# A two-layer decoder on one core: the last routing's softmax, counts and ranks placed behind the slot products, three row normalisations given to GpSimd, and two pieces per head in the last four heads

## The chip, the cores and the metric

The kernel runs on one core of a Trainium2 chip. The metric is device time in microseconds: the median of three runs. One execution was also taken by the hardware profiler, and its page and trace are what this document reads. PE is TensorE's matmul, PEld its weight load, DVE is VectorE, ACT is ScalarE, POOL is GpSimd and SP is SyncE, which issues most of the DMAs.

## The reference, cut to what matters

The program is a decoder of two layers over 16 batches of 112 tokens with 256 features, with a context of 375 rows per batch. Each layer is self attention, cross attention and a mixture of experts. The change lies at the end of layer 1's cross attention and the start of its experts:

```python
# layer 1, experts: E = 8 experts, top 2, capacity 33 slots per batch and expert
logits = einsum('btc,ce->bte', x, router_w) + router_b
top_k_logits, expert_indices = top_k(logits, 2)
expert_probs = softmax(top_k_logits)
one_hot = one_hot(expert_indices, first choices before second choices)
pos = cumsum(one_hot, axis=0) * one_hot - 1          # place of a token in its expert's queue
expert_inputs = zeros((E, 33, C)).at[expert, pos].add(x)
h = expert_inputs @ w_c_fc + b_c_fc ;  g = expert_inputs @ w_gate + b_gate
o = silu(h * g) @ w_c_proj + b_c_proj
x = x + sum_k expert_probs[k] * o[expert_k, pos_k]
```

In the actual reference, x at this place is the layer's residual, and a place beyond the capacity is dropped on the way in and clamped to the last slot on the way out.

## The kernel before, in words

The residual `x` stays in SBUF as 112 partitions (tokens) by 16 batches by 256. The stages run one after the other, and all of them are built from matmuls with f32 operands whose results go through eight PSUM banks, handed out in turn by `bank()`. A bank that has not been emptied by DVE or ACT holds the next matmul that wants it.

**Cross attention of layer 1.** A loop of 32 units goes over 16 batches and two halves of the heads (`n`, `b`, `u`; a unit is called a head below). In each unit, PE turns the softmax of this unit (`turned`, L1493), computes the scores of the next unit (`scores`, L1461), then does pieces of other work, and last the values of this unit (`values`, L1509). DVE takes the row maxima (L1472) and reciprocals of the sums (L1482), ACT takes the exponentials (L1473), and POOL scales the four rows of probabilities (L1484), two after each reciprocal. The other pieces are: context normalisation and K, V and Q of the next batch (no K and V in heads before batches 4, 8 and 12, for which they were made earlier), the output product of the batch before (`project`, which adds into `x` at L1315 and takes statistics at L234 and L235; POOL makes the inverse deviation with L242 and L243, and DVE normalises at L238), its transposes into `xnT` (L267, L269), and one entry of the list `after`.

**The list `after`.** It holds functions, and each head pops one. `routed(b)` computes the router's logits of a batch (`logits1`, L1219). With every fourth batch it also runs `route1`, which takes the two largest logits of four batches (`top_two`, L297 to L305), the softmax of the two (L1227 to L1231), and returns `places`. `places` multiplies the one-hots by a triangular matrix on PE and then works on DVE: the position (L1250), the expert (L1252), whether it fits (`ok`, L1253), the clamped position `kept` (L1255), the slot number `place` (L1257 to L1259), and how many tokens lie beyond the first 12 slots (`more`, L1261, added to `need` at L1264). `dispatch1(b)` makes a 112x264 row of slots (`slot_rows`, L1285 and L1286), normalises the rows of the batch (L238), multiplies them on PE (L1275) and copies the result into `first_in` (first 12 slots of each expert) and `more_in` (the rest), once by DVE and once by ACT (L1278, L1279). What is still in the list behind the last head is done there, and the last routing, of batches 12 to 15, at the start of the expert stage.

**Experts.** The expert stage works by units of eight slots (`hidden(n, j)`): four matmuls (L120), one ACT step (L1766), one DVE product (L1767) and, for every second slot, a Silu. Units `(0, e)` take the first 12 slots of an expert, units `(1, r)` the remaining 21 of the expert of rank `r`. `ranks()` sorts the experts by `need`; its result is first used by the weight load and the biases of unit 2. A list `jobs` holds DVE work that fits beside the matmuls: biases by rank (`bias_of`), and the share matrices of the output (`share_jobs`). One job is popped per slot.

**What sets the order.** In the cross attention, only PE keeps the order in which the code issues (`manual_schedule` with PE alone); DVE's, ACT's and POOL's orders are set by a scheduler from its own estimate when the program is built. In the expert stage, PE and DVE keep the order of the code. Each engine then takes its queue strictly in order, whatever waits at its head.

Of the kernel before, what the change touches and what calls it, by code (L numbers as in the profile page):

```python
# [9 lines left out]
F32 = mybir.dt.float32  # L10
U32 = mybir.dt.uint32
AF = mybir.ActivationFunctionType
ALU = mybir.AluOpType
# [16 lines left out]
P0 = 12  # L30
# [8 lines left out]
def _constants():  # L39
# [28 lines left out]
        "rev16": rows(E0 - np.arange(E0)),  # L68
        "rev8": rows(E1 - np.arange(E1)),
        "io8": rows(np.arange(E1)),  # L70
        "slots": rows(np.arange(E1 * CAP)),

        "later": np.concatenate(
            [
# [24 lines left out]
def tile_decoder(ctx: ExitStack, tc: tile.TileContext, t: dict, out: bass.AP):  # L99
# [1121 lines left out]
    def route1(lp, q):  # L1221

        bs = slice(4 * q, 4 * q + 4)
        (oh0, v0), (oh1, v1) = top_two(lp, lg1[:, bs, :], E1, const("rev8", L))

        p0, ex = prob[0][:, bs], prob[1][:, bs]
        nc.vector.tensor_sub(ex, v1, v0)  # L1227
        nc.scalar.activation(ex, ex, AF.Exp)
        nc.vector.tensor_scalar(p0, ex, 1.0, None, ALU.add)
        nc.vector.reciprocal(p0, p0)  # L1230
        nc.vector.tensor_mul(ex, ex, p0)  # L1231

        oh = [o.rearrange("p b n -> p (b n)") for o in (oh0, oh1)]

        def places():
            pc = bank()
            before = const("before", L)
            mm_sum(pc[:L, : 4 * E1], [(before, oh[0])])
            mm_sum(pc[:L, 4 * E1 : 8 * E1], [(before, oh[1]), (ones[:L, :L], oh[0])])
            b1 = lambda name: lp.tile([L, 4], F32, tag=f"rt_{name}", name=name, bufs=1)  # L1240
            tmp = lp.tile([L, 4, E1], F32, tag="rt_tmp", name="tmp", bufs=1)
            sums = lp.tile([L, E1], F32, tag="rt_sums", name="sums", bufs=1)
            for k in range(2):
                pos, ok, more = b1(f"pos{k}"), b1(f"ok{k}"), b1(f"more{k}")
                o3 = (oh0, oh1)[k]
                kept, ei = pos1[k][:, bs], exp1[k][:, bs]
                nc.vector.tensor_tensor(
                    tmp, o3, pc[:L, 4 * k * E1 : 4 * (k + 1) * E1].rearrange("p (b n) -> p b n", n=E1), ALU.mult
                )
                nc.vector.tensor_reduce(pos, tmp, AX.X, ALU.add)  # L1250
                nc.vector.tensor_tensor(tmp, o3, over(const("io8", L), 4), ALU.mult)
                nc.vector.tensor_reduce(ei, tmp, AX.X, ALU.add)  # L1252
                nc.vector.tensor_scalar(ok, pos, CAP - 0.5, None, ALU.is_lt)  # L1253

                nc.vector.tensor_scalar(kept, pos, float(CAP - 1), None, ALU.min)  # L1255

                nc.vector.scalar_tensor_tensor(pos, ei, float(CAP), kept, ALU.mult, ALU.add)  # L1257
                nc.vector.scalar_tensor_tensor(pos, pos, 1.0, ok, ALU.add, ALU.mult)
                nc.vector.tensor_scalar(place[k][:, bs], pos, -1.0, None, ALU.add)  # L1259

                nc.vector.tensor_scalar(more, kept, P0 - 0.5, None, ALU.is_gt)  # L1261
                nc.vector.tensor_tensor(tmp, o3, bcast(more, E1), ALU.mult)
                nc.vector.tensor_reduce(sums, tmp.rearrange("p b n -> p n b"), AX.X, ALU.add)
                nc.vector.tensor_add(need, need, sums)  # L1264

        return places

    def dispatch1(lp, b, made=None):

# [8 lines left out]
            copy(first_in[:, c, :, :, b], src[:, :, :P0])  # L1278
            copy(more_at[:, c, :, :, b], src[:, :, P0:])  # L1279

    def slot_rows(lp, b):
        slots = const("slots", L)
        dm = lp.tile([L, E1 * CAP], F32, tag="dm", name="dm", bufs=2)
        d1 = lp.tile([L, E1 * CAP], F32, tag="d1", name="d1", bufs=1)
        nc.vector.tensor_scalar(d1, slots, place[0][:, b : b + 1], None, ALU.is_equal)  # L1285
        nc.vector.scalar_tensor_tensor(dm, slots, place[1][:, b : b + 1], d1, ALU.is_equal, ALU.add)  # L1286
        xn = lp.tile([L, D], F32, tag="xn", name="xn", bufs=2)
        normed(xn, x[:, b, :], mv1[:, b, 0:1], r1[:, b : b + 1])
        return dm, xn


# [5 lines left out]
    with ExitStack() as ph:  # L1297
# [243 lines left out]
        with tc.manual_schedule(engines={mybir.EngineType.PE}):  # L1541
# [48 lines left out]
            def routed(b):  # L1590
                logits1(b)
                if b % 4 == 3:
                    q = b // 4
                    places = route1(rp, q)
                    after.append(places)
                    if q < B // 4 - 1:
                        after.extend(lambda b=b: dispatch1(lp, b) for b in range(4 * q, 4 * q + 4))

            units = [(b, u) for b in range(B) for u in range(2)]
            for n, (b, u) in enumerate(units):  # L1600
# [8 lines left out]
                if b + 1 in AHEAD and u == 0:  # L1609
                    k_load(b + 1)  # L1610
                    v_load(b + 1)
                if after:
                    after.pop(0)()
                if late and n:
                    flush(0)
                    if b:
# [29 lines left out]
    with ExitStack() as ph:  # L1646
# [261 lines left out]
```

## Time and profile before

| quantity | value |
|---|---|
| time, median of 3 runs | 1604.29 us (1603.69 to 1607.48) |
| the profiled execution's own time | 1611.35 us |
| span in the profile | 1609.6 us, mean granted clock 0.973 |
| PE, DVE, ACT, POOL busy | 1501.8, 964.1, 577.9, 483.1 us |
| last scores of the cross attention (L1461) | 1298.65 us from the span's start |
| last logits (L1219) | 1325.21 us |
| first slot row of the last routing (L1285) | 1333.43 us |
| first expert matmul | 1342.73 us |

The span is what the trace covers; the profiled execution took 1.75 us more than its span and about 7 us more than the median of the runs. A row of the timeline gives the start in us, the duration, the engine, the line of the kernel, the operation and, in brackets, how long the engine had been idle and what ended that. Durations of several instructions merged in a row are from the first start to the last end.

### The profile page before, as it was taken

How to read it: one execution, taken by the hardware profiler on the slowest of the kernel's cores; microseconds unless marked ns; L12 is line 12 of the kernel's file. 1: busy time of each engine (PE TensorE's matmuls, PEld its weight loads, DVE VectorE, ACT ScalarE, POOL GpSimd, SP SyncE). 2: the span in 40 equal slices, each digit the busy share in tenths (PEclk: the TensorE clock that was granted, in tenths of full speed). 3: DMA queues.
4: the chain of work that ended last, by engine and by line, in shares of the span. 5: the costliest groups of instructions: out<-in, count | busy, mean ns of one | idle time of the engine just before them, and what ended most of it. 6: DMA issues, size and time to landing. Idle time of an engine off the chain costs nothing.

```text
span 1609.6 us, 30346 instructions
## 1 busy us (share of the span) xinstructions
PE 1501.8 (93%) x11438; PEld 1127.5 (70%) x11438; DVE 964.1 (60%) x2649; ACT 577.9 (36%) x1437; POOL 483.1 (30%) x647
## 2 busy tenths in 40 slices
PE   7898999999988896899999989999999978999998
PEld 5776777777754585778888756666666657788786
DVE  6986777777762353976677655566575566342124
ACT  3441444444442252223333233343434323333332
POOL 5642122222115352323333344544445420000000
PEclk9999999999999897999999999999999988999999
DMA  6500322222224476200000010101010012344421
GB/s 170 143 10 21 94 67 65 67 65 65 64 76 158 130 231 214 54 24 1 1 1 2 20 56 10 49 20 48 19 30 30 1 53 79 137 178 157 147 89 48
DMA packets 84929, 116.52 MB, mean 72 GB/s; under 512 B 13433, under 2 KB 70946, under 8 KB 84778
## 3 DMA queue, kind: packets, MB, share of 16 engines
q1 hardware_dynamic: 78690, 98.25, 20.1%
q0 software_dynamic: 3312, 8.54, 1.6%
q10 hardware_dynamic: 2776, 7.72, 1.4%
q8 instruction: 95, 1.56, 0.4%
q14 instruction: 56, 0.46, 0.1%
HBM read 84.41 MB, written 22.08 MB: 66 GB/s over the span
## 4 chain that ended last, share of the span: by engine, by line
PE 76%; DVE 13%; POOL 4%; DMA 3%; issue 2%; another core or an unknown queue 1%; ACT 1%; SPq 0%; POOLq 0%; DVEq 0%; ACTq 0%
PE pT L120 49%; PE pT L785 3%; PE pT L1461 3%; PE pT L1493 2%; POOL pr L1484 2%; DVE mx L769 2%; PE pT L1509 2%; PE pT L803 2%; PE pT L767 2%; PE pT L1358 2%; PE pT L1393 2%; PE pT L1379 2%; PE pT L620 1%; DVE st L234 1%
## 5 line engine op out<-in xcount | busy, mean ns | idle before, releaser
L1484 POOL TENSOR_SCALAR pr<-pr,den 112x375 f32<-112x375 f32 x128 | 157.0, 1244 | 176.9 <-DVE den L1482 157.7
L120 PE MATMUL pT<-xnT,w_all 128*128 128x224 f32 (+2 forms) x800 | 165.3, 358 | 0.6 <-DVE xnT L269 0.5
L120 PEld LDWEIGHTS pT<-xnT,w_all 128*128 128x128 f32 x800 | 145.9, 197 | 10.2 <-issue 5.7
L794 ACT ACTIVATE pr<-pT 125x336 f32<-125x336 f32 x256 | 94.6, 456 | 126.3 <-PE pT L785 126.3
L769 DVE TENSOR_REDUCE mx<-pT 112x1 f32<-112x375 f32 x256 | 122.2, 539 | 11.3 <-PE pT L767 9.9
L1371 POOL TENSOR_TENSOR pr<-pr,den 112x448 f32<-112x448 f32 x64 | 59.9, 956 | 198.8 <-DVE den L1369 147.9
L120 PE MATMUL pT<-w_all 128*128 (+3 forms) x376 | 113.1, 453 | 1.7 <-ACT w_all L392 0.8
L120 PE MATMUL pT<-w_all,cT 128*125 128x256 f32 (+1 forms) x336 | 111.4, 475 | 0.0
L120 PE MATMUL pT<-cT,w_all 128*128 128x375 f32 x320 | 110.2, 486 | 0.0
L120 PE MATMUL pT<-w_all,xnT 128*112 128x256 f32 (+1 forms) x320 | 105.7, 477 | 1.9 <-ACT xnT L566 0.9
L120 PE MATMUL pT<-w_all,oT 128*112 128x256 f32 x448 | 106.4, 383 | 0.6 <-DVE oT L1400 0.6
L242 POOL TENSOR_SCALAR nr<-nmv 112x1 f32<-112x1 f32 x96 | 22.3, 232 | 273.7 <-DVE nmv L235 273.1
L1308 ACT COPY pT<-pT 112x448 f32<-112x448 f32 (+1 forms) x64 | 34.0, 532 | 170.9 <-PE pT L1493 88.3
L120 PEld LDWEIGHTS pT<-w_all 128*128 128x128 f32 (+2 forms) x376 | 70.2, 190 | 33.8 <-issue 4.6
L1473 ACT ACTIVATE pr<-pT,top 112x375 f32<-112x375 f32 x128 | 72.4, 572 | 56.8 <-DVE top L1472 54.4
L120 PEld LDWEIGHTS pT<-cT,w_all 128*128 128x128 f32 x320 | 59.3, 190 | 41.1 <-issue 5.8
L120 PEld LDWEIGHTS pT<-w_all,oT 128*112 128x112 f32 x448 | 75.7, 177 | 16.3 <-DVE oT L1400 1.0
L120 PE MATMUL pT<-first_in,w_all 128*128 128x192 f32 x512 | 86.6, 329 | 0.0
L120 PEld LDWEIGHTS pT<-first_in,w_all 128*128 128x128 f32 x512 | 84.4, 192 | 1.5 <-issue 0.3
L120 PEld LDWEIGHTS pT<-w_all,cT 128*125 128x125 f32 x336 | 61.1, 187 | 33.3 <-issue 22.7
L120 PEld LDWEIGHTS pT<-w_all,xnT 128*112 128x112 f32 x320 | 57.1, 183 | 35.8 <-issue 22.4
L1767 DVE SCALAR_TENSOR_TENSOR hT<-pT,vT,gt 128x192 f32<-128x192 f32 x64 | 26.7, 417 | 90.5 <-ACT gt L1766 90.4
(306 smaller groups left out, 3019.2 us busy)
## 6 DMA issues: line engine op xcount, KB each, us to landing
w_all<-in_L_ffn_w_c_fc_dram SPq DMA_DIRECT2D x12, 1024.0 KB
w_all<-in_L_ffn_w_gate_dram SPq DMA_DIRECT2D x12, 1024.0 KB
w_all<-in_L_ffn_w_c_proj_dram SPq DMA_DIRECT2D x12, 1024.0 KB
cx<-in_ctx_dram SPq DMA_DIRECT2D x32, 375.0 KB
kz<-kn SPq DMA_DIRECT2D x128, 46.9 KB
xg<-w_all SPq DMA_DIRECT2D x1, 5547.0 KB
xb<-xg SPq DMA_DIRECT2D x36, 129.0 KB
yb<-yo SPq DMA_DIRECT2D x16, 224.0 KB
```

The lines of the kernel that those rows point to most:

```text
L120: mm(o, l, r, start=(i == 0), stop=(i == len(terms) - 1))
L767: mm(ps[i][:L, :S], qz[b % 2][r, g, :], kz[b % 2][r, g, :], start=True, stop=True)
L769: nc.vector.tensor_reduce(mx[b % 2][:, g, i, 16:17], ps[i][:L, :S], AX.X, ALU.max, negate=True)
L785: mm(pw[i][:KC, j * L : (j + 1) * L], kz[b % 2][r, g, j * KC : (j + 1) * KC], qm[r, :], start=True, stop=True,)
L794: nc.scalar.activation(pr[:, i, :], pw[i][:KC, : NKC * L], AF.Exp)
L803: mm(po[32 * i : 32 * i + 32, :L], va[b % 2][:, j, 4 * g + i, :], pr[:, i, j * L : (j + 1) * L], start=(j == 0), stop=(j == NKC - 1),)
L1308: nc.scalar.copy(dst, src)
L1358: mm(ps[k][:L, s * L : (s + 1) * L], q, kk, start=True, stop=True)
L1371: nc.gpsimd.tensor_tensor(pr[:, k], pr[:, k], bcast(den[:, k, :], L), ALU.mult)
L1461: mm(ps[2 * s + k][:L, :S], qTs[b // 2][rows(k), m, (b % 2) * L : (b % 2 + 1) * L], kTs[b][rows(k), m, :], start=True, stop=True,)
L1473: nc.scalar.activation(pr[:, i, :], ps[i][:L, :S], AF.Exp, bias=top[:, i : i + 1], scale=1.0, accum_out=den[:, i : i + 1],)
L1484: nc.gpsimd.tensor_scalar(pr[:, n, :], pr[:, n, :], den[:, n : n + 1], None, ALU.mult)
```

## The change

- The slot constant gets one more entry, and slot numbers count from 1, so that a token that doesn't fit has number 0 and no subtraction of 1 is needed. `place` is made from the unclamped position and `ok`.
- `kept`, the clamped position, is computed by POOL.
- `route1` returns two functions. `places` keeps what the slot rows need. `counts` has the softmax, `more`, and the sums into `need`. For the first three routings, `counts` is an entry of `after` of its own, behind the four dispatches. For the last one it is the first entry of `jobs`, in the first slot of the first expert unit.
- From head 28 on, two entries of `after` are popped per head.
- At the start of the expert stage, POOL normalises the rows of batches 12, 13 and 14 (into three buffers); for batch 15, the copy that its transposes read is used.
- `ranks()` moves from in front of the last dispatches into the jobs, as the fifth, followed by the biases of rank 0.

```diff
-        "slots": rows(np.arange(E1 * CAP)),
+        "slots": rows(np.arange(E1 * CAP + 1)),
...
-        p0, ex = prob[0][:, bs], prob[1][:, bs]
-        nc.vector.tensor_sub(ex, v1, v0)
-        nc.scalar.activation(ex, ex, AF.Exp)
-        nc.vector.tensor_scalar(p0, ex, 1.0, None, ALU.add)
-        nc.vector.reciprocal(p0, p0)
-        nc.vector.tensor_mul(ex, ex, p0)
...
-                nc.vector.tensor_scalar(kept, pos, float(CAP - 1), None, ALU.min)
-
-                nc.vector.scalar_tensor_tensor(pos, ei, float(CAP), kept, ALU.mult, ALU.add)
-                nc.vector.scalar_tensor_tensor(pos, pos, 1.0, ok, ALU.add, ALU.mult)
-                nc.vector.tensor_scalar(place[k][:, bs], pos, -1.0, None, ALU.add)
-
-                nc.vector.tensor_scalar(more, kept, P0 - 0.5, None, ALU.is_gt)
-                nc.vector.tensor_tensor(tmp, o3, bcast(more, E1), ALU.mult)
+                to = place[k][:, bs]
+                nc.vector.scalar_tensor_tensor(to, ei, float(CAP), pos, ALU.mult, ALU.add)
+                nc.vector.scalar_tensor_tensor(to, to, 1.0, ok, ALU.add, ALU.mult)
+
+                nc.gpsimd.tensor_scalar(kept, pos, float(CAP - 1), None, ALU.min)
+
+        def counts():
+
+            p0, ex = prob[0][:, bs], prob[1][:, bs]
+            nc.vector.tensor_sub(ex, v1, v0)
+            nc.scalar.activation(ex, ex, AF.Exp)
+            nc.vector.tensor_scalar(p0, ex, 1.0, None, ALU.add)
+            nc.vector.reciprocal(p0, p0)
+            nc.vector.tensor_mul(ex, ex, p0)
...
+            for k in range(2):
+                more = b1(f"more{k}")
+                nc.vector.tensor_scalar(more, pos1[k][:, bs], P0 - 0.5, None, ALU.is_gt)
+                nc.vector.tensor_tensor(tmp, (oh0, oh1)[k], bcast(more, E1), ALU.mult)
                 nc.vector.tensor_reduce(sums, tmp.rearrange("p b n -> p n b"), AX.X, ALU.add)
                 nc.vector.tensor_add(need, need, sums)
 
-        return places
+        return places, counts
...
-    def slot_rows(lp, b):
-        slots = const("slots", L)
+    def slot_rows(lp, b, xn=None):
+        slots = const("slots", L)[:, 1:]
...
-        xn = lp.tile([L, D], F32, tag="xn", name="xn", bufs=2)
-        normed(xn, x[:, b, :], mv1[:, b, 0:1], r1[:, b : b + 1])
+        if xn is None:
+            xn = lp.tile([L, D], F32, tag="xn", name="xn", bufs=2)
+            normed(xn, x[:, b, :], mv1[:, b, 0:1], r1[:, b : b + 1])
...
-                    places = route1(rp, q)
+                    places, counts = route1(rp, q)
                     after.append(places)
                     if q < B // 4 - 1:
                         after.extend(lambda b=b: dispatch1(lp, b) for b in range(4 * q, 4 * q + 4))
+                    after.append(counts)
...
-                if after:
-                    after.pop(0)()
+                for _ in range(2 if n > 27 else 1):
+                    if after:
+                        after.pop(0)()
...
             late.pop(0)()
-            while after:
+            xns = {}
+            for b in range(B - 4, B - 1):
+                xns[b] = lp.tile([L, D], F32, tag="xn", name="xn", bufs=3)
+                nc.gpsimd.tensor_scalar(
+                    xns[b], x[:, b, :], mv1[:, b, 0:1], r1[:, b : b + 1], ALU.subtract, ALU.mult
+                )
+            xns[B - 1] = xn15
+            after.pop(0)()
+            while len(after) > 1:
                 after.pop(0)()
-            made = {b: slot_rows(lp, b) for b in (B - 4, B - 3)}
-            ranked = ranks()
+            made = {b: slot_rows(lp, b, xns[b]) for b in (B - 4, B - 3)}
             for b in range(B - 4, B):
                 dispatch1(lp, b, made.pop(b))
                 if b + 2 < B:
-                    made[b + 2] = slot_rows(lp, b + 2)
-            jobs = bias_of(0)
-            jobs += share_jobs(share_first, KA, first_idx)
+                    made[b + 2] = slot_rows(lp, b + 2, xns[b + 2])
+            ranked = []
+            jobs = [after.pop(0)] + share_jobs(share_first, KA, first_idx)
+            jobs.insert(4, lambda: ranked.extend(ranks()))
+            jobs[5:5] = bias_of(0)
```

More of the change, by code (lines that the diff above doesn't have):

```diff
@@ L1241, in places @@
             tmp = lp.tile([L, 4, E1], F32, tag="rt_tmp", name="tmp", bufs=1)
-            sums = lp.tile([L, E1], F32, tag="rt_sums", name="sums", bufs=1)
             for k in range(2):
-                pos, ok, more = b1(f"pos{k}"), b1(f"ok{k}"), b1(f"more{k}")
+                pos, ok = b1(f"pos{k}"), b1(f"ok{k}")
                 o3 = (oh0, oh1)[k]
@@ L1253, in places @@
                 nc.vector.tensor_scalar(ok, pos, CAP - 0.5, None, ALU.is_lt)
-                nc.vector.tensor_scalar(kept, pos, float(CAP - 1), None, ALU.min)
-                nc.vector.scalar_tensor_tensor(pos, ei, float(CAP), kept, ALU.mult, ALU.add)
-                nc.vector.scalar_tensor_tensor(pos, pos, 1.0, ok, ALU.add, ALU.mult)
-                nc.vector.tensor_scalar(place[k][:, bs], pos, -1.0, None, ALU.add)
-                nc.vector.tensor_scalar(more, kept, P0 - 0.5, None, ALU.is_gt)
-                nc.vector.tensor_tensor(tmp, o3, bcast(more, E1), ALU.mult)
+                to = place[k][:, bs]
[9 more added lines that the diff above has]
+            nc.vector.tensor_mul(ex, ex, p0)
+            b1 = lambda name: lp.tile([L, 4], F32, tag=f"rt_{name}", name=name, bufs=1)
+            tmp = lp.tile([L, 4, E1], F32, tag="rt_tmp", name="tmp", bufs=1)
+            sums = lp.tile([L, E1], F32, tag="rt_sums", name="sums", bufs=1)
+            for k in range(2):
+                more = b1(f"more{k}")
+                nc.vector.tensor_scalar(more, pos1[k][:, bs], P0 - 0.5, None, ALU.is_gt)
+                nc.vector.tensor_tensor(tmp, (oh0, oh1)[k], bcast(more, E1), ALU.mult)
                 nc.vector.tensor_reduce(sums, tmp.rearrange("p b n -> p n b"), AX.X, ALU.add)
                 nc.vector.tensor_add(need, need, sums)
-        return places
+        return places, counts
     def dispatch1(lp, b, made=None):
```

## The prediction

> **What bounds the kernel now.** I read the page first (busy rows, slices), then busy time by stretch, then the timeline of the stretches that the edit touches, and last the changed program's order of instructions on each engine with what each waits for.
>
> The page says that TensorE sets the pace nearly everywhere:
>
> ```profile
> span 1609.6 us, 30346 instructions
> PE 1501.8 (93%) x11438; PEld 1127.5 (70%) x11438; DVE 964.1 (60%) x2649; ACT 577.9 (36%) x1437; POOL 483.1 (30%) x647
> PE   7898999999988896899999989999999978999998
> PEclk9999999999999897999999999999999988999999
> ```
>
> PE is at 93%; the one dip late in the run, the digits 7 and 8 after the long row of nines, is the seam between the cross attention and the expert stage, and PEclk falls there too. By stretch (first column us, then PE, PEld, DVE, ACT, POOL busy with counts, granted clock, DMA share, GB/s):
>
> ```profile
> 1209.00:1217.70 8.70, 8.70 (x66) 6.81 (x65) 4.63 (x14) 4.31 (x14) 5.33 (x6) 1.00 0.20 83
> 1217.70:1227.80 10.10, 8.14 (x59) 5.59 (x58) 6.28 (x17) 4.17 (x14) 5.29 (x5) 1.00 0.00 0
> 1307.50:1310.30 2.80, 0.00 (x0) 0.02 (x1) 2.60 (x9) 0.00 (x0) 0.16 (x1) 0.50 0.00 0
> 1310.30:1314.80 4.50, 4.49 (x31) 3.56 (x31) 2.98 (x9) 0.61 (x2) 0.00 (x0) 0.56 0.03 5
> 1325.20:1333.40 8.20, 1.51 (x6) 1.27 (x6) 6.73 (x42) 0.20 (x1) 0.00 (x0) 0.50 0.00 0
> 1333.40:1342.70 9.30, 6.90 (x18) 4.75 (x19) 8.21 (x32) 1.81 (x6) 0.00 (x0) 0.68 0.00 1
> 1342.70:1346.50 3.80, 3.80 (x17) 3.52 (x17) 0.51 (x2) 1.02 (x3) 0.00 (x0) 0.70 0.00 0
> ```
>
> At 1325 to 1333 PE does 1.5 of 8.2 us while DVE runs without pause: the last routing. Behind an idle stretch PE comes back at about half clock for some 4.5 us (0.56). And the short heads (no context pieces to make) hang on GpSimd: of 10.1 us PE is busy 8.1. The marks that I count from, in the timeline:
>
> ```profile
> 1212.29 4.86 POOL L1484 TENSOR_SCALAR pr<-pr,den 112x375 f32<-112x375 f32 x4 [4.99 <-DVE den L1482]
> 1222.27 5.00 POOL L1484 TENSOR_SCALAR pr<-pr,den 112x375 f32<-112x375 f32 x4 [4.27 <-DVE den L1482]
> 1301.79 4.94 POOL L1484 TENSOR_SCALAR pr<-pr,den 112x375 f32<-112x375 f32 x4 [6.07 <-DVE den L1482]
> 1310.31 2.10 PE L1275 MATMUL pT<-dm,xn 112*128 112x264 f32 x4 [2.94 <-DVE xn L238]
> 1325.21 0.17 DVE L1219 TENSOR_TENSOR lg<-pT,router_b 112x8 f32<-112x8 f32 x1 [1.01 <-PE pT L120]
> 1328.89 0.19 DVE L1247 TENSOR_TENSOR tmp<-oh,pT 112x32 f32<-112x32 f32 x1
> 1333.43 0.36 DVE L1285 TENSOR_SCALAR d<-call,place 112x264 f32<-112x264 f32 x1
> 1342.73 13.05 PE L120 MATMUL pT<-first_in,w_all 128*128 128x192 f32 x72
> ```
>
> So the last logits stand at 1325.21 and the first expert matmul starts at 1342.73, 17.5 us later. That is the stretch the edit shortens.
>
> **Part 1: the last routing (gain).** Times from the last logits on. Top-two is unchanged; its second one-hot is ready at +2.6, the counting matmul behind it is done at +3.65, and the first product (L1247) starts at +3.7. The five softmax steps lay inside that wait (1327.77 to 1328.77), so taking them out gains 0.1 at most. Then 26 DVE steps took 1328.89 to 1333.43 = 4.5; now 14 remain (two of 26 go to GpSimd, eight into the piece counts, the others are folded), at the same spacing of 0.18 on average: 2.5. Slot rows start at +6.2, not +8.2. Behind them, 1333.43 to 1342.73 = 9.3 holds two blocks that leave DVE: four row normalisations (0.41 each; three go to GpSimd, batch 15 uses its copy) and eleven rank steps (1335.68 to 1337.82 = 2.1), which held up the first copy out of PSUM. What is left is first slot row 0.9, then eight dispatch matmuls on a cold PE, the first four or so at 0.93 (3.70 for four here), then near 0.45, with copies of 0.75 per batch between: I get +12.8 for the first expert matmul. Gain 17.5 - 12.8 = 4.7. As PE then has run 5 us without a gap, the first expert slot should be warm, where now 1342.7 to 1346.5 has clock 0.70 (3.8 x 0.3 = 1.1 lost): gain 0.7, between 0 and 1.1.
>
> **Part 2: what is put behind.** Softmax, counts, ranks become jobs of the first expert unit: 13, then 11 DVE steps of 0.2, plus one exp on ACT (0.2, before the Silu table is loaded, so no extra table load). DVE in that unit: eight products of 0.42 (3.4), counts 2.6, two index jobs 1.0, shares 1.1, ranks 2.3, biases 1.4: 11.8 against 11.6 of PE (36 matmuls at 0.36 less the cold start). It lags, but eight banks let PE run three slots ahead and I find no slot whose product comes late: 0. If that cover fails: up to 2. The ranks' consumer on SP, the load of unit 2, waits for unit 0's weights to be free anyway: 0. The `need` matmul is queued on PE behind slot 4 and the counts are done by then: 0. The constants are one column longer: 0.
>
> **Part 3: `kept` by GpSimd, and who waits (loss).** In the heads, `kept` stands in GpSimd's queue between and behind the scalings of the head, and DVE's `more` (reads `kept`) stands in DVE's queue right after `ok`, before the second reciprocal, the rest of the places, the slot rows and the evacuations. So DVE waits for two scalings (2.45), then GpSimd waits for DVE, then DVE waits for the next two. Counted from the end of the head's first reciprocal: first `kept` +2.85, second reciprocal +3.45 (now about +1.3), scalings end +5.95 (now +5.0), second `kept` +6.2, slot rows +8.1.
> Routing 0 falls into a long head. Its second reciprocal stands ahead of the wait, evacuations come 2.6 late, but the banks are wanted only at about that time: +0.5, between 0 and 2.
> Routing 1: one queue place per routing now goes to the counts, so it slides from a long head to the short one at 1209. There the row's inverse deviation is also behind `kept` on GpSimd, so the two normalisations end at +9.1, the output copy at +9.75, the two transposed copies at +11.4 (now +6.95 and +8.1 to +8.2); the next head's maxima follow at 12 and its first reciprocal, which now also stands behind the fourth maximum, ends at 14.1 instead of 9.98. In this pair of heads GpSimd's scalings end last already (0.63 of PE waiting three times between 1223.7 and 1227.8), so all of it arrives at PE: 4.1 less what transposes catch up, +3.8. The long heads behind it are full on PE and give nothing back. Bounds: 0 if DVE's order hurts nothing, 5.
>
> **Part 4: doubled pieces in heads 28 to 31 (loss, then gain).** In head 30 places 2 *and* the first dispatch now come before project(14), values and the last transposes on PE's in-order queue. PE has its counting matmuls done at 1300.9 and then stands at the dispatch until the slot row is ready: first reciprocal 1301.63, `kept` 1304.5, second reciprocal 1305.1, second `kept` 1307.85, six steps and the row of 0.49: 1309.3. Today PE does 4.9 us of work meanwhile (1.97 + 1.37 + 1.56) and waits for the same dispatch until 1310.3. From 1309.3, cold for 4 us: dispatch 2.1, project 2.9, values 1.3, transposes 1.6 to 1317.3; second dispatch (its row normalised late) 1318.2 to 1319.1, third 1319.8 to 1320.7, transposes and values to 1322.5, project(15) to 1324.5, last dispatch to 1325.4. Two of the three dispatches that now follow project(15) are gone from there, which is counted.
> Then the rows by GpSimd: the new `xn` tiles lie where the old stage's tiles lay, and the first one waits for the last dispatch's matmul (1325.4); the three are ahead of batch 15's inverse deviation in the queue. No row shows a two-scalar subtract-multiply of 112x256 there; the nearest is L1484, 112x375 in 1.244, which scales to 0.85. GPSIMD Engine Reference, section 4.1 of the Trainium skill, advises VectorE for elementwise work but calls one-input work on GpSimd roughly line rate; the page's best loop, about 1.8 cycles per element at 1.2 GHz, would make it 0.38 (estimate from that page). The trace's row, 3.3 ns per element, speaks against it, so I take 0.85: three make 2.55, and the deviation ends at 1328.9 instead of 1327.2. By the page the sum below would be 1.4 lower. Bounds 0.38 and 1.24.
> Then normalise, transpose, copy, logits as today (2.05 from transposes to logits): 1331.4. That is 6.2 later than 1325.21, between 3 and 9.
>
> **Sum.** +0.5 +3.8 +6.2 -4.7 -0.7 = +5.1. The profiled execution took 1611.35 (span 1609.6 and 1.75 around it); it becomes 1616.5. The runs' median, 1604.29, is 7 lower; the same shift gives 1609.4 (+0.32%).
>
> **Rivals.**
> A, the waits are covered: DVE has slack (60%), so routing 1 costs under 1, and the late heads lose only what the two dispatches save, 1 to 2. For it: DVE idles 3.4 us for L238 in that very head today, and PE would pass through dispatch 8 at almost the same time as now. Against it: work of 4.9 us that filled that hole now stands behind it. It decides if logits come less than 3 us later: -5.4 + 2 = about -3.5, 1600.8; not slower.
> B, DVE becomes the bound of the first expert unit as well, or GpSimd's rows take 1.2 and up: 24 small steps in two slots, and the outputs of unit 0 wait for the last Silu. For it: 11.8 against 11.6. Against: deep banks. +3 to +6 more, 1613.5.
> C, the edit doesn't do what it says: the doubled pops only move two dispatches, as PE's order shows, and four pops go to the counts. That is inside the forecast.
>
> **How the numbers follow.** A difference under 0.3% (4.8 us) is about what measurements of this kernel cannot tell from none. Forecast, +1 to +9: 0.68 (slower by over 0.3% 0.43, within 0.25). A: 0.18 (faster 0.07, within 0.11). B: 0.14, slower. Sums: 0.07, 0.36, 0.57. The forecast's own range is 1605 to 1613.5; with most of A and B, 1602.5 to 1616.
>
> **What would show it.** Right: DVE waits for GpSimd at `more`, about 2 us twice, in three heads; a PE gap of about 8 us ahead of the first dispatch of batch 8; three GpSimd rows of 0.85 directly before the last L242; last logits to first expert matmul 12.8; clock 1.00 in the first expert slots. Wrong: no such gap (A), or DVE without idle time and PE waiting in the first expert unit (B).

## The result and the profile after

The changed kernel took 1614.96 us (median of 4, 1613.59 to 1618.11) against 1603.99 us for the kernel before in the same series (median of 4): a ratio of 1.0068, 95% interval 1.0046 to 1.0089. In a later series it was run again, unaltered: 1.0045, interval 1.0028 to 1.0061. It is slower, by 7 to 11 us; the forecast was 5.1, and the first median lies 1.5 us beyond the forecast's own range, which ended at 1613.5. (A ratio here is not exactly the quotient of the two medians; the two differ by up to 0.0007, or 1.1 us.)

The page of the changed kernel, the rows that answer to those shown of before:

```profile
span 1616.3 us, 30344 instructions
...
PE 1507.1 (93%) x11438; PEld 1131.2 (70%) x11438; DVE 960.3 (59%) x2629; ACT 578.4 (36%) x1437; POOL 488.3 (30%) x658
...
PE   7898999999989896999999989999998968999998
...
PEclk9999999999999998999999999899999987999999
```

The span is 6.7 us longer, and PE's busy time has grown by 5.3 of that. So the page alone doesn't say what the edit cost: 3.1 us lie in a head that it doesn't touch and that ran at a lower granted clock (see the last section). It has to be read by stretch. The seam between cross attention and experts now reads 8, 9, 6, 8 where it read 7, 8.

Busy time by stretch in the changed kernel (us, then PE, PEld, DVE, ACT, POOL with counts, granted clock, DMA share, GB/s). In order: the two heads around routing 1, the gap ahead of batch 8's dispatch, the stretch behind it, the last routing's chain, its dispatches, and the start of the experts:

```profile
1206.30:1215.70 9.40, 8.75 (x67) 6.76 (x66) 5.33 (x24) 3.94 (x12) 5.35 (x6) 1.00 0.20 80
1215.70:1228.20 12.50, 8.83 (x59) 5.93 (x58) 10.01 (x33) 3.90 (x13) 5.77 (x6) 0.97 0.00 0
1303.70:1311.90 8.20, 0.03 (x1) 0.06 (x1) 3.97 (x27) 1.76 (x6) 5.36 (x6) 0.63 0.00 0
1311.90:1316.40 4.50, 4.50 (x11) 3.42 (x12) 2.51 (x10) 0.61 (x2) 0.00 (x0) 0.53 0.00 0
1337.00:1344.00 7.00, 1.51 (x6) 1.27 (x6) 5.21 (x29) 0.00 (x0) 0.45 (x2) 0.50 0.00 0
1344.00:1350.90 6.90, 6.84 (x17) 5.11 (x17) 4.40 (x14) 1.82 (x6) 0.00 (x0) 0.55 0.00 0
1350.90:1354.70 3.80, 3.80 (x23) 3.65 (x24) 1.35 (x8) 1.64 (x5) 0.00 (x0) 1.00 0.00 0
```

And the whole way from the start of the last head's scores to the last logits, in the kernel before and in the changed one:

```profile
1298.65:1325.21 26.56, 19.80 (x123) 15.19 (x122) 18.07 (x69) 5.65 (x18) 6.59 (x8) 0.79 0.20 66
```

```profile
1301.46:1336.97 35.51, 20.38 (x123) 15.52 (x122) 16.93 (x64) 5.67 (x18) 10.56 (x13) 0.75 0.14 50
```

On this way PE is busy for about as long (20.4 us, 19.8 before), and the way is 9 us longer: what was added here is idle time. The head behind routing 1 has grown from 10.1 to 12.5 us, and PE has an empty stretch of 8.2 us that was 2.8. On the other side the last routing takes 6.1 us from the last logits to the first slot row (1336.97 to 1343.07) instead of 8.2, and the experts start at clock 1.00 instead of 0.70. The timeline of the same run shows what the empty times end on (`issue` stands where the profile shows nothing that the engine waited for):

```profile
1212.24 0.17 DVE L1267 TENSOR_SCALAR more<-pos 112x4 f32<-112x4 f32 x1 [1.90 <-POOL pos L1251]
1215.37 0.17 DVE L1267 TENSOR_SCALAR more<-pos 112x4 f32<-112x4 f32 x1 [1.37 <-POOL pos L1251]
...
1307.40 0.17 DVE L1267 TENSOR_SCALAR more<-pos 112x4 f32<-112x4 f32 x1 [1.90 <-POOL pos L1251]
1310.53 0.17 DVE L1267 TENSOR_SCALAR more<-pos 112x4 f32<-112x4 f32 x1 [1.79 <-POOL pos L1251]
1311.87 2.10 PE L1281 MATMUL pT<-dm,xn 112*128 112x264 f32 x4 [8.19 <-DVE dm L1292]
1329.83 3.65 POOL L1841 TENSOR_SCALAR xn<-x_res,mv,r 112x256 f32<-112x256 f32 x3 [10.93 <-PE pT L120]
1333.45 0.23 POOL L242 TENSOR_SCALAR r<-mv 112x1 f32<-112x1 f32 x1
1334.93 0.61 PE L267 MATMUL pT<-call,w_all 112*128 112x112 f32 x2 [4.86 <-DVE w_all L238]
1336.97 0.17 DVE L1219 TENSOR_TENSOR lg<-pT,router_b 112x8 f32<-112x8 f32 x1 [1.01 <-PE pT L120]
1340.65 0.19 DVE L1239 TENSOR_TENSOR tmp<-oh,pT 112x32 f32<-112x32 f32 x1 [1.05 <-PE pT L120]
1344.06 5.62 PE L1281 MATMUL pT<-dm,xn 112*128 112x264 f32 x12 [3.45 <-issue]
1350.86 6.89 PE L120 MATMUL pT<-first_in,w_all 128*128 128x192 f32 x40
```

VectorE (DVE) waits for GpSimd's (POOL's) `kept` twice in a routing, PE stands 8.19 us for the slot row behind that, and batch 15's inverse deviation (L242) starts only when three rows on GpSimd are through; PE stands 4.86 us for it.

The end of the program can be cut in three at marks that every kernel here has: the start of the last head's scores, the last logits, the first expert matmul. All in us, from the timelines; "heads" is how much later the last scores start than in the profile of before, less the same difference at the start of head 18 (from there to head 22, ahead of everything that the edit changes in routing 1, no kernel's difference moves by more than 0.01 us).

| kernel | heads | last scores to last logits | to first expert matmul | to the end |
|---|---|---|---|---|
| before | 0 | 26.56 | 17.52 | 266.9 |
| changed | +4.7 | 35.51 | 13.89 | 265.5 |
| changed, again | +3.1 | 35.58 | 13.91 | 265.5 |
| `kept` by VectorE | +2.8 | 32.23 | 14.04 | 265.6 |
| one piece per head | +4.2 | 29.20 | 14.05 | 266.1 |
| rows by VectorE | +3.1 | 31.80 | 12.55 | 265.6 |
| only the short last routing | -0.3 | 26.32 | 14.10 | 265.5 |
| ... with `kept` by GpSimd | +5.6 | 28.89 | 12.71 | 265.4 |
| ... with rows by GpSimd | -0.3 | 26.28 | 14.16 | 265.5 |
| ... with doubled pieces | +9.0 | 22.71 | 12.84 | 266.0 |
| ... with a held dispatch | +1.3 | 23.67 | 13.89 | 266.5 |
| ... held, rows by GpSimd | -0.3 | 23.98 | 13.50 | 266.9 |

Three things in the table are not the edits' doing, as far as the traces show:

- Four profiles (changed, `kept` by VectorE, one piece per head, held dispatch) ran head 25 at a granted clock of 0.87 to 0.90, where the others have 1.00; that is about 1.5 us in each of these "heads". The held dispatch leaves that head as it was before, so it isn't the change that brings it.
- Among the kernels behind before, "to first expert matmul" falls into two groups: about 12.7, where the last dispatches ran at a clock of 0.67 to 0.70, and about 14, where they had 0.54 to 0.58.
- "To the end" differs behind the last matmul: from the first expert matmul to the last one, every kernel but before takes 260.1 us (before: 261.0).

### The profile page after: what moved, and what is told of

It is laid out like the page before. It is cut to its first block, busy times and chain, and to the rows that moved or that the text cites. A ratio compares the mean times of both kernels' runs of the same rounds, so it can differ in the third digit from the quotient of the medians.

```text
span 1616.3 us, 30344 instructions
## 1 busy us (share of the span) xinstructions
PE 1507.1 (93%) x11438; PEld 1131.2 (70%) x11438; DVE 960.3 (59%) x2629; ACT 578.4 (36%) x1437; POOL 488.3 (30%) x658
## 4 chain that ended last, share of the span: by engine, by line
PE 78%; DVE 11%; POOL 5%; DMA 3%; issue 2%; ACT 1%; SPq 0%; POOLq 0%; ACTq 0%; DVEq 0%
PE pT L120 50%; PE pT L1468 3%; PE pT L785 3%; PE pT L1500 2%; POOL pr L1491 2%; DVE mx L769 2%; PE pT L1516 2%; PE pT L803 2%; PE pT L767 2%; PE pT L1365 2%; PE pT L1400 2%; PE pT L1386 2%; PE pT L620 1%; PE pT L1281 1%; DVE st L234 1%
## 5 line engine op out<-in xcount | busy, mean ns | idle before, releaser
L120 PEld LDWEIGHTS pT<-xnT,w_all 128*128 128x128 f32 x800 | 144.4, 195 | 10.1 <-issue 5.4
L242 POOL TENSOR_SCALAR nr<-nmv 112x1 f32<-112x1 f32 x96 | 22.3, 232 | 273.7 <-DVE nmv L235 273.1
L120 PE MATMUL pT<-hT,w_all 128*128 128x192 f32 (+1 forms) x384 | 79.7, 366 | 0.0
```

The costliest lines, as they stand in the source:

```text
L120: mm(o, l, r, start=(i == 0), stop=(i == len(terms) - 1))
```

## The experiments

The theory from the two traces: the gain at the last routing is there, and it is eaten by three new waits, on GpSimd's queue (`kept`), on the pieces pulled forward, and on the rows ahead of batch 15's inverse deviation. The rivals: the jobs moved into the first expert unit cost; or routing 1 loses because the longer list pushes it into a short head and not because of the wait. The ratios below are to the kernel before in the same series (1606.34, then 1607.26 and 1605.90 us).

**`kept` by VectorE again.**

```diff
-                nc.gpsimd.tensor_scalar(kept, pos, float(CAP - 1), None, ALU.min)
+                nc.vector.tensor_scalar(kept, pos, float(CAP - 1), None, ALU.min)
```

> The changed kernel with one word different: the minimum that makes `kept` is VectorE's again. Theory (VectorE waits for GpSimd's queue): the two waits of routing 1 (1.90 and 1.37 us) and those of routing 2 (1.90 and 1.79 us) at `more` go, two instructions of about 0.17 us come back per routing; routing 1 costs 1 us instead of about 4.3, the gap of TensorE before batch 8's dispatch shrinks from 8.2 to about 4.5 us, so about 6 us of the 11 are won back: near 1609. Rival (the wait is not the cause, the slide of routing 1 into a short head is): routing 1 keeps its 4 us, only some 2 us are won in head 30: near 1613. Rival (the jobs moved into the first expert unit cost): no change, 1615.

Measured: 1609.37 us, ratio 1.0024 (1.0013 to 1.0036), where the first expectation had put it. In its trace VectorE does not wait at `more`, and the gap ahead of batch 8's dispatch is shorter by 2.9 us:

```profile
1301.93 0.17 DVE L1267 TENSOR_SCALAR more<-pos 112x4 f32<-112x4 f32 x1
...
1303.08 2.10 PE L1281 MATMUL pT<-dm,xn 112*128 112x264 f32 x4 [5.25 <-DVE dm L1292]
```

Last scores to last logits fell from 35.5 to 32.2. Against the changed kernel's 1.0045 that is 3.4 us won, against its 1.0068, 7 us. The wait is a cause, but it isn't the only one: 5.25 us of the gap stay (4.5 had been expected), and the head behind routing 1 still takes 11.2 us (10.1 before).

**One piece per head.**

```diff
-                for _ in range(2 if n > 27 else 1):
+                for _ in range(1):
```

> The changed kernel with one piece per head in the late heads too; `kept` and the rows stay with GpSimd. The pieces left over (places of routing 2, four dispatches, counts) then run after the last projection. Theory: the 8.2 us gap before batch 8's dispatch and the cold stretch behind it go (about -6), but the places' chain (2.4 us) and eight matmuls of 0.5 to 0.9 us now stand between the last projection and the last routing (about +5): near 1614, no gain that can be measured. Rival (doubled pieces are the main loss and the leftover pieces hide under the waits of batch 15's normalisation): near 1609. Rival (doubling was worth something): 1618 or more.

Measured: 1606.64 us, ratio 1.0003 (0.9993 to 1.0012). The first expectation, no gain, was wrong; the second had the direction, and more was won than it gave. The trace says why it wins more than the doubling alone: with the places of routing 2 behind the last projection, GpSimd has no scalings left to stand in `kept`'s way, and the three rows now stand behind batch 15's inverse deviation, not ahead of it:

```profile
1311.66 0.23 POOL L242 TENSOR_SCALAR r<-mv 112x1 f32<-112x1 f32 x1 [8.24 <-DVE mv L235]
...
1313.07 0.17 DVE L1267 TENSOR_SCALAR more<-pos 112x4 f32<-112x4 f32 x1
...
1315.26 5.23 PE L1281 MATMUL pT<-dm,xn 112*128 112x264 f32 x12 [4.01 <-DVE dm L1292]
...
1322.27 0.39 PE L267 MATMUL pT<-call,w_all 112*128 112x112 f32 x2
1322.29 3.66 POOL L1841 TENSOR_SCALAR xn<-x_res,mv,r 112x256 f32<-112x256 f32 x3 [8.32 <-PE pT L1281]
```

So this run undoes three things at the end of the program at once, and a cleaner test of the doubling follows below. Its new price is in the same lines: batch 15's transposes (L267) stand behind four dispatches.

**Rows of batches 12 to 14 by VectorE.**

```diff
-                nc.gpsimd.tensor_scalar(
+                nc.vector.tensor_scalar(
                     xns[b], x[:, b, :], mv1[:, b, 0:1], r1[:, b : b + 1], ALU.subtract, ALU.mult
                 )
```

> The changed kernel with the rows of batches 12 to 14 made by VectorE at the same place in the program. Theory (batch 15's inverse deviation stands behind three rows of 1.22 us in GpSimd's queue): it comes about 3.3 us earlier, the three rows cost VectorE some 0.35 us each of which about half delays the logits: last scores to last logits from 35.5 to about 33 us, the whole near 1612.3. Rival (the rows only fill time in which the projection and cold matmuls are late anyway): 1615, and the gap before batch 15's transposes stays at 4.9 us with another engine named.

Measured: 1609.32 us, ratio 1.0024 (1.0013 to 1.0035). In its trace the inverse deviation starts as soon as its variance is there, and PE's wait for the transposes is 1.43 us instead of 4.86:

```profile
1320.72 0.23 POOL L242 TENSOR_SCALAR r<-mv 112x1 f32<-112x1 f32 x1 [11.11 <-DVE lg L1219]
...
1322.19 0.38 PE L267 MATMUL pT<-call,w_all 112*128 112x112 f32 x2 [1.43 <-DVE w_all L238]
```

The stretch from the last scores to the last logits fell by 3.7 us where 2.5 were expected. The one behind it fell by another 1.35, which the edit did not set out to win: the last dispatches ran at a granted clock of 0.70 instead of 0.55 (stretch of the dispatches in this kernel):

```profile
1330.90:1336.40 5.50, 5.50 (x16) 3.92 (x16) 4.15 (x14) 1.82 (x6) 0.00 (x0) 0.70 0.00 0
```

**Only the shortened last routing.** The three edits above together, and the counts of the first three routings in one piece with their places, so that the list of pieces has its old length and routings 1 and 2 stay in their old heads:

```diff
-                    after.append(places)
+                    after.append(places if q == B // 4 - 1 else lambda: (places(), counts()))
...
-                    after.append(counts)
+                    else:
+                        after.append(counts)
```

> Of the changed kernel only the shortened last routing is kept: `kept` and the rows are VectorE's, one piece per head in all heads, and in the first three routings the counts run in one piece with the places, so that the list of pieces is no longer than before. Theory (the losses are the wait, the doubled pieces, the slide and the rows; the split last routing brings 17.5 to about 13 us between last logits and first expert matmul, and a warm first slot): 1604 - 4.5 - 0.7 + 0.5 = about 1599.5. Rival (counts and ranks in the first expert unit cost as much as they save): 1604. Rival (moving the softmax, which is now behind the places in every routing, delays the heads): 1606 or more.

Measured: 1602.56 us, ratio 0.9976 (0.9967 to 0.9985): 3.8 us faster than before, where the first expectation gave 4.7. The heads lose nothing, the stretch to the logits is the old one, and last logits to first expert matmul is 14.1 instead of 17.5. The jobs in the first expert unit therefore cost nothing that shows: from the first expert matmul to the last matmul it takes 0.9 us less than before, not more.

**The same with `kept` by GpSimd.**

```diff
-                nc.vector.tensor_scalar(kept, pos, float(CAP - 1), None, ALU.min)
+                nc.gpsimd.tensor_scalar(kept, pos, float(CAP - 1), None, ALU.min)
```

> The shortened last routing alone (one piece per head, counts in one piece with the places, rows by VectorE), with one thing taken back: `kept` is GpSimd's again, so VectorE's `more` waits for it in each of the first three routings. Theory (VectorE waits out GpSimd's queue): waits of 1 to 2 us stand at `more` again, routings 1 and 2 lose together 3 to 5 us against the same kernel without: ratio to before about 0.9976 + 0.0025 = 1.000. Rival (the wait only hurts in the short head to which the longer list had pushed routing 1; in the long head it is covered): 0.998, and the heads' starts keep their difference.

Measured: 1607.98 us, ratio 1.0007 (0.9995 to 1.0020), 5 us over the kernel without this line. Here routing 1 lies in a long head, where PE has other work, and it loses all the same. The timeline of that head:

```profile
1185.23 0.17 DVE L1267 TENSOR_SCALAR more<-pos 112x4 f32<-112x4 f32 x1 [1.90 <-POOL pos L1251]
...
1188.36 0.17 DVE L1267 TENSOR_SCALAR more<-pos 112x4 f32<-112x4 f32 x1 [1.79 <-POOL pos L1251]
...
1194.38 1.59 PE L1468 MATMUL pT<-kt,qt 64*112 64x375 f32 x2 [1.92 <-DVE vt L1454]
```

The last of these lines is the way the wait reaches PE: behind `more` VectorE's evacuations are late, among them that of a value piece (`vt`), and the next head's last two scores wait for it. That head takes 17.5 us instead of 11.6. Only 1.92 of the 6 us are idle time; the rest is slower matmuls, because behind the gap the granted clock is 0.50 for 6.6 us. The head up to the end of the gap, the stretch behind it and the remainder:

```profile
1190.94:1194.38 3.44, 1.52 (x8) 0.63 (x7) 3.44 (x12) 0.26 (x1) 0.00 (x0) 0.97 0.00 0
1194.38:1201.02 6.64, 6.64 (x12) 3.48 (x13) 5.33 (x15) 2.94 (x10) 3.20 (x3) 0.50 0.00 0
1201.02:1208.46 7.44, 7.44 (x50) 4.69 (x49) 2.40 (x4) 1.22 (x3) 2.09 (x2) 1.00 0.04 7
```

Idle time in smaller parts does not always cost clock: in the repeat of the changed kernel PE is idle for 3.7 us of head 24, in gaps of up to 1.29 us, and that head and the next run at 1.00. How often the clock falls behind the one gap of 1.92 us, a single profile doesn't tell. So a long head is no sure cover. It can be one: routing 0 lies in a long head too, VectorE waits there for `kept` in the changed kernel (1.48 and 0.87 us), and the heads lose nothing.

**The same with the rows by GpSimd.** Again against the kernel with only the shortened last routing:

```diff
-                nc.vector.tensor_scalar(
+                nc.gpsimd.tensor_scalar(
                     xns[b], x[:, b, :], mv1[:, b, 0:1], r1[:, b : b + 1], ALU.subtract, ALU.mult
                 )
```

> The shortened last routing alone, with the rows of batches 12 to 14 given back to GpSimd. Here they stand behind batch 15's inverse deviation in GpSimd's queue and wait for the last of the earlier dispatches. Theory (the rows cost in the changed kernel by their place ahead of that inverse deviation, not by being GpSimd's): nothing is lost, VectorE is free of 1.05 us before the last logits: 0.3 to 0.7 us faster than with VectorE's rows, ratio about 0.997. Rival (rows of 1.2 us on GpSimd are slow enough to hold the dispatch of batches 12 to 14, or GpSimd's work slows VectorE beside it): 1 to 3 us slower, 0.9985.

Measured: 1602.93 us, ratio 0.9969 (0.9955 to 0.9983), no difference from rows by VectorE. The rows are as slow as in the changed kernel, but stand behind the inverse deviation. They run beside batch 15's transposes and logits (the last logits are at 1318.18) and are done at 1318.8, long before the first slot row at 1324.35:

```profile
1311.54 0.23 POOL L242 TENSOR_SCALAR r<-mv 112x1 f32<-112x1 f32 x1 [10.70 <-DVE mv L235]
...
1315.14 3.68 POOL L1842 TENSOR_SCALAR xn<-x_res,mv,r 112x256 f32<-112x256 f32 x3 [2.72 <-DMA w_all<-in_L_ffn_w_c_proj_dram]
```

It is the place in the queue that cost, not the engine.

**The same with doubled pieces.** Against the same kernel:

```diff
-                for _ in range(1):
+                for _ in range(2 if n > 27 else 1):
```

> The shortened last routing alone (`kept` and rows by VectorE, counts in one piece with the places), with one thing of the change put back: two pieces in each head after the 27th. Its list is shorter by one piece than the changed kernel's, so routing 2 falls a head earlier (behind head 29's scores). Theory (doubled pieces put a routing's chain and its dispatches ahead of work that TensorE has ready): TensorE waits 4 to 5 us for batch 8's first rows, in exchange only one dispatch and no wait for it stands behind the last projection (26.3 us from last scores to last logits falls to 23 or 24): near the time without doubling, ratio 0.998 to 0.999. Rival (in the changed kernel doubling cost 6 us of itself): 1.001 or more. Rival (doubling is a gain once the list is short): 0.996.

Measured: 1607.90 us, ratio 1.0005 (0.9990 to 1.0020), 4.7 us over the kernel without. With the shorter list, routing 2 comes a head earlier than in the changed kernel, and PE waits there for the first slot row:

```profile
1288.24 2.10 PE L1281 MATMUL pT<-dm,xn 112*128 112x264 f32 x4 [5.25 <-DVE dm L1292]
...
1290.51 5.13 PE L120 MATMUL pT<-w_all,cT 128*125 128x512 f32 x8
```

The next scores start 9.2 us later than they did: the gap of 5.25, the dispatch's own time, and slow matmuls behind the gap (eight of 128x512 took 5.13 us here, 3.61 at full clock in before). Of that 3.6 us come back before the last logits, since fewer dispatches stand behind the last projection. Another 1.3 come back behind the last logits, but there the work is the same; the clock of the last dispatches was 0.67 instead of 0.55, as with the rows by VectorE:

```profile
1330.86:1336.44 5.58, 5.58 (x17) 4.10 (x17) 4.08 (x14) 1.84 (x6) 0.00 (x0) 0.67 0.00 0
```

The rest stays lost. The wait is the one expected first, but its price is not: the ratio lies between the first expectation and the second.

**A version to beat both.** Only the shortened last routing, with `kept` moved into the counts, and with batch 11's dispatch held until after the last logits, so that batch 15's transposes don't stand behind it in PE's queue:

```diff
-                nc.vector.tensor_scalar(kept, pos, float(CAP - 1), None, ALU.min)
+                at.append(pos)
...
+                nc.vector.tensor_scalar(pos1[k][:, bs], at[k], float(CAP - 1), None, ALU.min)
                 nc.vector.tensor_scalar(more, pos1[k][:, bs], P0 - 0.5, None, ALU.is_gt)
...
-        while len(after) > 1:
+        while len(after) > 4:
             after.pop(0)()
...
+            after.pop(0)
+            xh = lp.tile([L, D], F32, tag="xn_held", name="xn", bufs=1)
+            normed(xh, x[:, B - 5, :], mv1[:, B - 5, 0:1], r1[:, B - 5 : B - 4])
+            held = slot_rows(lp, B - 5, xh)
             late.pop(0)()
...
-            after.pop(0)()
+            for _ in range(3):
+                after.pop(0)()
+            dispatch1(lp, B - 5, held)
```

> A version meant to beat both: the shortened last routing alone, with `kept` in the counts, and with batch 11's dispatch held back behind the last logits, so that batch 15's transposes no longer stand behind it in TensorE's queue. Theory: in the run without this, the transposes began 3.3 us after the normalised rows were there (behind a 2.0 us wait for batch 11's rows, its 1.25 us and 1.5 us of logits); they now begin at once, the held dispatch fills part of TensorE's wait for the top two, and VectorE loses 0.6 us to making it; the places lose two instructions (0.4): about 2.5 us faster than 0.9976, so 0.996. Rival (VectorE's chain is what ends last, and the held dispatch's rows and copies only lengthen it): 0.998 or above.

Measured: 1597.87 us, ratio 0.9941 (0.9926 to 0.9956): 9.4 us faster than before, and faster than forecast. The transposes wait for their rows alone, and the held dispatch runs inside PE's wait for the one-hots:

```profile
1318.66 0.38 PE L267 MATMUL pT<-call,w_all 112*128 112x112 f32 x2 [1.24 <-DVE w_all L238]
...
1320.40 1.89 PE L1284 MATMUL pT<-dm,xn 112*128 112x264 f32 x4
```

Last scores to last logits is 23.7 instead of 26.3, 2.6 us less, as forecast. The two ratios, from different series, differ by 0.35%, which is 5.6 us; the near ends of their intervals are 1.8 us apart, so 2.6 is possible. No trace shows where more would come from. Two things were changed here at once, but ahead of the last logits `kept` in the counts moved nothing: batch 8's dispatch starts 11.4 us after the last scores with it and without it.

**The held dispatch, with the rows by GpSimd.**

```diff
-                nc.vector.tensor_scalar(
+                nc.gpsimd.tensor_scalar(
                     xns[b], x[:, b, :], mv1[:, b, 0:1], r1[:, b : b + 1], ALU.subtract, ALU.mult
                 )
```

> The best version so far (shortened last routing, `kept` in the counts, batch 11's dispatch held behind the last logits) with the rows of batches 12 to 14 by GpSimd, behind batch 15's inverse deviation in its queue. Theory: VectorE's 1.05 us ahead of the last logits go, GpSimd's 3.7 us of rows end before the places do: up to 0.7 us faster than with VectorE's rows, ratio about 0.994, no difference that can be measured. Rival: GpSimd's rows end late and hold batch 12's dispatch: 1 to 2 us slower, 0.995.

Measured: 1599.87 us, ratio 0.9958 (0.9943 to 0.9974). The two intervals overlap: no difference that can be told, as expected.

## Why the prediction was right, and where its sizes were off

The direction, the mechanism and the place of each wait were right; the size was too small. The sum was +5.1. By the table the traces give +8.7 in the first profile (heads +4.7, to the logits +9.0, to the first expert matmul -3.6, behind it -1.4) and +7.2 in the second (+3.1, +9.0, -3.6, -1.4). The difference is the clock of heads 24 and 25 (0.96 and 0.90 in the first, 1.00 in the second), 1.6 us. The ratios say 11 us in the first series and 7.2 in the second: the second agrees with its trace, and of the first some 2 us stay unexplained. That the sum came as near as it did is in part luck: it had the routings in the heads 1.2 too high and the gain behind the last logits 0.4 too high, and the late heads 2.8 too low.

- *Routing 0, +0.5.* It was 0.0: VectorE waits there (1.48 and 0.87 us at `more`), but the heads' starts keep their difference to the kernel before across it.
- *Routing 1, +3.8.* From head 22 to head 29 the starts fell back by 4.2 us in the first profile, 1.6 of it the clock of heads 24 and 25. The second profile, without that, gives 2.6. The forecast put all of it on the wait for `kept`. The runs split it: the short head that holds the routing takes 9.4 us with the wait (the repeat), 8.65 without, and 8.6 where routing 1 stays a head earlier (the shortened routing alone, and before); the head behind it 12.15, 11.2 and 10.1. So over the two heads the wait costs 1.8 us, and the slide, for which the prediction gave no price of its own, 1.1.
- *Late heads, +6.2.* It was +8.95. Batch 8's dispatch came 10.4 us after the last scores, where 10.65 had been worked out, so the mechanism and its largest part were right. Three terms were too small. The path from there to the end of the last dispatch took 17.5 us instead of 16.1, so that this end came 1.15 us later than worked out (27.9 against 26.75 from the last scores). The first row on GpSimd started 0.46 us after that end (1329.83 against 1329.37), where nothing had been put. And a row takes 1.22 us, not 0.85: three take 3.65, not 2.55. The row of 112x375 had been scaled down by its elements; unscaled, 1.24, it would have been right, and it was named as the bound.
- *The rule weighed there.* The 0.38 us for a row was an estimate from the best case of about 1.8 cycles per element in the Trainium skill, GPSIMD Engine Reference, section 3.1. The trace's 1.22 decides: this operation takes three times as long. The prediction sided with the trace and then still trusted the scaling too far.
- *Last logits to first expert matmul, -4.7.* It was -3.6. The places were as worked out (2.4 us from the first product at 1340.65 to the first slot row at 1343.07). The dispatches were not: they had been put at 0.93 for the first four and then near 0.45, but in the changed kernel PE was cold (at a low granted clock) through all of them (0.55, 12 matmul instructions in 5.62 us). In the run with rows by VectorE, where the clock was 0.70, the stretch took 12.55, within 0.3 of the predicted 12.8.
- *Warm first slot, -0.7.* To the last matmul it was -0.9 (261.0 to 260.1 us), near the forecast: clock 1.00 instead of 0.70 over 3.8 us is 1.1 of it. The other 0.5 of the -1.4 lies behind the last matmul.
- *Jobs in the first expert unit, 0.* Shown by the run of the shortened routing alone, and there is more room than was worked out: in the changed kernel VectorE is busy for 8.7 of the unit's 12.2 us, not 11.8 of 11.6.

Rival A (the waits are covered) falls in the changed kernel's own trace: the logits come 9 us later from the last scores, where it gave 1 to 2 for the late heads, and routing 1 costs more than 1 us. It was right for routing 0 alone. Rival B fell in its first half (no loss in the first expert unit). The second half, rows of 1.2 us, came true, but not at its price: the rows took 1.1 us more than forecast, not 3 to 6, so its 1613.5 is close to the first median by luck. Rival C holds that the doubled pieces only move two dispatches. They are moved, but not for nothing: doubling alone costs 4.7 us.

The parts don't add: taking back one alone from the changed kernel won 3.4 (`kept`), 3.4 (rows) and 6.7 us (doubling) against the repeated run, each with an uncertainty of about 3 us. They meet in the same queues, and the third undoes part of the others. What each is worth in other combinations, and how much of the 7 to 11 us is the slide of the routings alone, was not measured further.

## What to carry to other kernels

A small instruction given to an engine that is mostly idle costs what stands ahead of it in that engine's queue, and the engine that waits for its result passes the wait on to everything behind it: 0.22 us of work on GpSimd cost up to 1.9 us per wait and 5 us per run (in that run's profile, partly by the lower clock behind the gap). Before moving work, read for both engines what is next to it in the queue; the same three rows cost 3.4 us ahead of an inverse deviation and nothing that shows behind it. And on an in-order engine, pulling a piece forward is a loss if its input comes later than the work that it jumps ahead of; holding one back until a known wait shortened its stretch by 2.6 us here.

## What the runs showed of the hardware

The span of one profile says less than it seems to: two profiles of the identical changed kernel had spans of 1616.3 and 1609.6 us, the second equal to that of the kernel before. Of the 6.7 us, 2.5 lie ahead of the first head, 2.7 in heads 0 to 17 and 1.6 in heads 24 and 25. A good part of the 2.7 is head 9, where only the granted clock differs. The same head in before, the changed kernel, its repeat and the shortened routing alone (us, PE busy, granted clock, DMA share, GB/s), where PE has no idle time in any:

```profile
1045.60:1058.20 12.60, 12.60 (x76) 0.90 0.10 32
```

```profile
1041.00:1056.70 15.70, 15.70 (x77) 0.72 0.08 26
```

```profile
1039.30:1052.40 13.10, 13.10 (x77) 0.87 0.10 31
```

```profile
1035.80:1051.50 15.70, 15.70 (x75) 0.71 0.08 26
```

So differences of a few us between spans were read stretch by stretch, with the clock beside them, and what is faster or slower was taken from the ratios over many runs.

The second surprise was GpSimd: subtract and multiply with two per-row scalars on 112x256 takes 1.22 us, as long as one multiply on 112x375 (1.24 us), so neither the elements alone nor the number of operations alone gives its price, and 112x4 takes 0.22 us. Nor is it the number of tensors read: adding two tensors of 112x256 (TENSOR_TENSOR) takes 0.73 us, less than the row that reads one. The groups of the changed kernel (after the count: busy us, mean ns of one, idle time before them):

```profile
L1491 POOL TENSOR_SCALAR pr<-pr,den 112x375 f32<-112x375 f32 x128 | 156.8, 1241 | 181.9 <-DVE den L1489 155.1 <-PE pT L120 19.6 <-PE pT L1281 7.3
L1841 POOL TENSOR_SCALAR xn<-x_res,mv,r 112x256 f32<-112x256 f32 x3 | 3.6, 1217 | 10.9 <-PE pT L120 10.9
L485 POOL TENSOR_TENSOR x_res<-x_res,bo 112x256 f32<-112x256 f32 x16 | 11.6, 726 | 0.0
L1251 POOL TENSOR_SCALAR pos<-pos 112x4 f32<-112x4 f32 x8 | 1.8, 224 | 8.0 <-DVE pos L1242 7.7
```

On VectorE, the same three rows take 0.41 us each.
